# A convolution, attention and expert kernel: both attention stages in fixed orders, and the first image's table in one go

## The chip, the cores and the metric

The kernel runs on one core of one Trainium2 chip. The metric is the device time of the whole program in microseconds (us), the median over several runs. A core has a matrix engine (PE, with its weight loads PEld), a vector engine (DVE), a scalar engine (ACT), a general engine that also issues the indirect transfers (POOL), an engine that issues plain transfers (SP), and 16 DMA engines. TensorE's clock is granted by a throttle, and the profile gives the granted share.

## The reference

Four images of 256 channels and 64 x 64 positions pass two layers, all in float32.

```
x = x + deformable_conv(group_norm(x))        # 3 x 3 taps, offsets and masks from a convolution
t = tokens(x)                                 # 4 x 4096 tokens of 256 channels
t = t + attention(layer_norm(t))
t = t + experts(layer_norm(t))                # 8 experts, the best 2 of each token
```

The convolution samples, for each position and tap, four neighbours with bilinear weights. The attention works across the 4 images, not across positions: for each of 8 heads of 32 channels, the scores of image s against image t are sums over all 4096 positions, the softmax is over the 4 images, and the values are mixed by 4 x 4 numbers for each head, gated by a sigmoid, and projected with a bias. `layer_norm` is applied twice in a row ahead of the projections (once outside, once inside the attention). Experts are a 256 to 256 to 256 network with an exact gelu.

## The kernel before

**Prologue and gathers (layer 0).** Each image gets a table in DRAM, whose rows hold a position and the one below it side by side. `pieces(b)` builds it: group statistics, `block(q)` for each of 8 blocks of 512 positions, which normalizes (`norm`), transposes (`turn`), copies to one of two staging buffers `zt` (`leave`), and issues four stores of 256 KB; the same `block` computes the offsets by a convolution (`rows_of`, `shifted`, `summed`, `kept`), and `positions` turns them into row numbers and weights. For image 0 all this has to be done ahead of the first gather, except the offsets of blocks from `EARLY` = 3 on. Images 1 to 3 are done beside the gathers. `routed` then multiplies the 18 weight blocks of the convolution with the expert router's 8 columns, so that the convolution's products also give its output's router logits; hence rows of `CR` = 264 columns.

The main loop makes 1152 steps (32 tiles of 128 positions x 9 taps x 4 images). In each, POOL issues one indirect gather of 128 rows into one of `NGB` = 10 buffers `g`, ACT and DVE weigh the four corners (`corner0`, `corner`), PE transposes the sum and multiplies it (`product`), adding on the image itself. `done` stores the tokens into `t1` in DRAM in 32 pieces (image b, block j) of 512 tokens. The order of DVE, ACT, PE and POOL is written out by hand here.

**First attention stage.** A loop over 8 blocks of 512 positions j and 4 images b, in an order that the framework's scheduler decides. It loads `t1[b][j]` whole, takes statistics on DVE (`layernorm`), a reciprocal root as a power on POOL (`rstd_of`), and normalizes on DVE:

```
for i in range(NT):
    V.tensor_scalar(dst[:, i, :], src[:, i, :], mv[:, i, 0:1], r[:, i : i + 1], ALU.subtract, ALU.mult)
```

PE transposes it, ACT scales it into the state in SBUF (`channel_major`), PE projects it to q and k (two halves of channels each), ACT copies them. After the four images of a j, DVE makes 32 products `junk<-q,k` that sum up the scores. When all is done a small softmax gives `att`, 4 x 4 numbers for each channel. Ahead of the loop, `routed` multiplies the output weights `wo_sb` with the router, too.

**Second attention stage.** `block(j)` for 8 blocks, in an order that is written out for DVE, ACT and PE. For the four images it does: `value` (two PE projections; for the first image ACT spreads them, scaled, over four buffers `mix`), `mixed` (DVE adds the others), `gate` (a projection and a sigmoid), `gated` (DVE), `output` (PE, 264 columns), `residual` (loads `t1` again and adds the output's bias `bo_sb` on DVE), `added` (DVE, into the state, with a copy to `t2` in DRAM for the first half), then `stats` (DVE `bn_stats` and `bn_aggr`, a power on POOL for each image), `shift`, and `normed` (ACT, into scatter buffers `u`, 6 of them). `pick`, `count` and `placed` choose the two experts and the place of each token in the expert's list. These three for block j-1 run within block j. Then POOL issues 32 scatters of 128 rows for a block, in pieces 14, 4, 4, 5 and what is left. All of block j-1's scatters are issued within block j. After block 4 come `plan(0)` and `fill(0)`, after block 5 `experts_in` (the loads of all expert weights), each in one piece.

**Experts.** 142 tiles of 256 rows, in two halves of the blocks, in a fixed order: rows and weights are fetched, two products each, and the result is scattered back. The last block's `normed`, `pick`, `count`, `placed` and `plan(1)` are put between the first tiles, and its 32 scatters go out one a tile. The tail gathers the two results of each token, weighs, transposes and stores the output.

Of the kernel before, what the change touches and what calls it, by code (L numbers as in the profile page):

```python
# [17 lines left out]
P = 128  # L18
# [14 lines left out]
CR = C + NE  # L33
# [10 lines left out]
EARLY = 3  # L44
# [26 lines left out]
def conv_attn_moe_kernel(  # L71
# [32 lines left out]
    nhalf = const.tile([P, 4], F32, name="nhalf")  # L104
# [28 lines left out]
    def routed(rows, rw, ps_turned, ps_out, pool, name):  # L133


        pr = ps_out.tile([P, len(rows), NE], F32, name=f"{name}_pr", tag="om")
        for n, w in enumerate(rows):
            tp = ps_turned.tile([P, C], F32, name=f"{name}_tp{n}", tag="tp")
            for ch in range(NCH):
                T.transpose(tp[:, ch * P : (ch + 1) * P], w[:, ch * P : (ch + 1) * P], ident)  # L140
            wT = pool.tile([P, C], F32, name=f"{name}_wT{n}", tag="sT")
            S.copy(wT, tp)
            for ch in range(NCH):
                T.matmul(
                    pr[:, n, :], wT[:, ch * P : (ch + 1) * P], rw[:, ch, :],
                    start=(ch == 0), stop=(ch == NCH - 1),
                )
        for n, w in enumerate(rows):
            V.tensor_copy(w[:, C:], pr[:, n, :])

    issued = []

    def in_turn(ins, others):

        for other in others:
            tc.add_manual_dep(
                ins.ins, other.ins.name,
                mybir.DependencyInfo(mybir.DependencyClass.NoSync, mybir.DependencyReason.DATA),
                reason="order of issue",
            )  # L160

    def rstd_of(pool, var, n, name, twice=False, into=None):
# [7 lines left out]
        r = into  # L170
        if into is None:
            r = pool.tile([P, n], F32, name=f"{name}_rstd", tag=f"rstd{n}")
# [26 lines left out]
    with ExitStack() as actx:  # L199
        aw = actx.enter_context(tc.tile_pool(name="a_w", bufs=1))  # L200
        ax = actx.enter_context(tc.tile_pool(name="a_x", bufs=2))
        apad = actx.enter_context(tc.tile_pool(name="a_pad", bufs=2))
        ap_ = actx.enter_context(tc.tile_pool(name="a_params", bufs=2))
        atmp = actx.enter_context(tc.tile_pool(name="a_tmp", bufs=1))
        ag = actx.enter_context(tc.tile_pool(name="a_gather", bufs=1))
        asm = actx.enter_context(tc.tile_pool(name="a_sm", bufs=5))
        ast = actx.enter_context(tc.tile_pool(name="a_stage", bufs=2))
        ps_tp = actx.enter_context(tc.tile_pool(name="ps_tp", bufs=4, space=PSUM))
# [6 lines left out]
        def load_image(b):  # L215
            t = ax.tile([P, NCH, HW], F32, name=f"xraw{b}", tag="xraw")
# [34 lines left out]
        rwc_sb = load_weight(aw, router_w, "rwc_sb")  # L251
# [35 lines left out]
        def pieces(b):  # L287
# [51 lines left out]
            def block(q, at, table=True, offsets=True, alone=False):  # L339
# [9 lines left out]
                def norm(ch):  # L349
                    if ch == 0:  # L350
                        t["xs"] = apad.tile(
                            [P, NCH, RB + 2, W], F32, name=f"xs{b}_{q}{between}",
                            tag=f"xs{between}", bufs=2 if table else 1,
# [7 lines left out]
                    if alone and table:  # L361
                        V.tensor_scalar(to, of, scale, bias, ALU.mult, ALU.add)
                    else:
                        S.activation(to, of, AF.Identity, bias=bias, scale=scale)
# [11 lines left out]
                def leave(i):  # L376
                    if i == 0:
                        t["zt"] = ast.tile([P, NT, C], F32, name=f"zt{b}_{q}", tag="zt")
                    zt = t["zt"]
                    S.copy(zt[:, i, :], t["tp"])  # L380
# [51 lines left out]
                each = 2 if alone else 4  # L432
                if table:
                    for i in range(NT):
                        out_.append((at + each - 1 + each * i, lambda i=i: turn(i)))
                        out_.append((at + each + each * i, lambda i=i: leave(i)))
                sum_at = at + (13 if alone else 18)
                if offsets:
                    for m in range(NCH * 3):
                        rows_at = at + 2 + 2 * m if alone else at + 4 + 2 * m + m // 2  # L440
                        out_.append((rows_at, lambda m=m: rows_of(m)))
                    for kj in range(3):
                        out_.append((sum_at + kj, lambda kj=kj: shifted(kj)))
                    out_.append((sum_at + (3 if alone else 4), lambda: summed(0)))
                    out_.append((sum_at + (4 if alone else 5), lambda: summed(1)))
                    out_.append((sum_at + (5 if alone else 6), kept))
# [100 lines left out]

            place_for()
            for q in range(NBLK):
                first.extend(block(q, n + 6 * q, offsets=False, alone=True))  # L550
            for q in range(EARLY):
                at = n + 9 + 12 * q
                first.extend(block(q, at, table=False, alone=True))
                first.extend(positions(rows_in(q), lambda q=q: of[q], at + 19, 2))
# [19 lines left out]
        ss, tps, sTs, accs, outs, last_corner = {}, {}, {}, {}, {}, {}  # L574
# [5 lines left out]
        def gather(n):  # L580
# [11 lines left out]
            tc.add_to_no_dep_group(buffer, g.ins)  # L592
            return g
# [66 lines left out]
        for when, fn in pieces(0):  # L660
            todo.setdefault(when, []).append(fn)
        routed(
            [wconv_sb[:, ch, k, :] for k in range(K2) for ch in range(NCH)], rwc_sb, ps_tp, ps_om,
            asm, "wconv",
        )
        order = {nc.vector.engine, nc.scalar.engine, nc.tensor.engine, nc.gpsimd.engine}
        with tc.manual_schedule(engines=order):
# [51 lines left out]
        [  # L719
            early_state[:, (j * B + b) * STATE : (j * B + b + 1) * STATE] if j < HB  # L720
            else state_pool.tile([P, STATE], F32, name=f"st{b}_{j}")
            for j in range(NBLK)
        ]
        for b in range(B)
    ]
    t2 = {
# [20 lines left out]
    att_pool = ctx.enter_context(tc.tile_pool(name="att", bufs=1))  # L747
    att = att_pool.tile([P, NCH, B, B], F32, name="att")

# [9 lines left out]
    route_pool = ctx.enter_context(tc.tile_pool(name="route", bufs=1))  # L759
# [4 lines left out]
    rw_sb = load_weight(dw, router_w, "rw_sb")  # L764
# [12 lines left out]
    with ExitStack() as bctx:  # L777
# [7 lines left out]
        wq_sb = load_weight(bw, wq, "wq_sb")  # L785
        wk_sb = load_weight(bw, wk, "wk_sb")
        with ExitStack() as ectx:
            et = ectx.enter_context(tc.tile_pool(name="e_t", bufs=1))
            ps_e = ectx.enter_context(tc.tile_pool(name="ps_e", bufs=1, space=PSUM))
            routed([wo_sb[:, ch, :] for ch in range(NCH)], rw_sb, ps_tp, ps_e, et, "wo")  # L790

            alike = et.tile([P, NCH, P], F32, name="alike")
            V.tensor_copy(alike, bo_c.unsqueeze(2).to_broadcast([P, NCH, P]))
            pb = ps_e.tile([P, 2, NE], F32, name="pb", tag="om")
            for n in range(2):
                for ch in range(NCH):
                    T.matmul(
                        pb[:, n, :], alike[:, ch, :] if n == 0 else ones, rw_sb[:, ch, :],
                        start=(ch == 0), stop=(ch == NCH - 1),
                    )  # L800
            V.tensor_copy(bo_sb[:, C:], pb[:, 0, :])
            V.tensor_copy(rsum, pb[:, 1, :])
# [3 lines left out]
        for j in range(NBLK):  # L806
            qs, ks = [], []
            for b in range(B):
                rows = bt.tile([P, NT, CR], F32, name=f"bt{b}_{j}", tag="t")
                nc.sync.dma_start(rows, t1[b][j])  # L810
                t = rows[:, :, :C]
                layernorm(bs, t, t, f"l1_{b}_{j}", twice=True)
                mn = channel_major(b, j)
                for ch, tp in transpose_in(ps_tp, t, f"tpb{b}_{j}"):
                    S.activation(
                        mn[:, ch, :], tp, AF.Identity,
                        scale=gamma_c[:, ch : ch + 1], bias=beta_c[:, ch : ch + 1],
                    )
                q = bqk.tile([P, NCH, BLK], F32, name=f"q{b}_{j}", tag="qk")
                k = bqk.tile([P, NCH, BLK], F32, name=f"k{b}_{j}", tag="qk")  # L820
                for w, dst, n in ((wq_sb, q, "q"), (wk_sb, k, "k")):
                    for ch in range(NCH):
                        S.copy(dst[:, ch, :], project(ps_mm, w, mn, ch, f"p{n}{b}_{j}_{ch}"))  # L823
                qs.append(q)
                ks.append(k)
            for s_ in range(B):
                for t_ in range(B):
                    for ch in range(NCH):
                        junk = bs.tile([P, BLK], F32, name=f"junk{s_}{t_}{ch}_{j}", tag="junk")
                        V.scalar_tensor_tensor(  # L830
                            junk, qs[s_][:, ch, :], 1.0, ks[t_][:, ch, :],
                            ALU.mult, ALU.mult,
                            accum_out=parts[:, ch, s_ * B + t_, j : j + 1],
                        )


# [82 lines left out]
    ps_s = ctx.enter_context(tc.tile_pool(name="ps_sd", bufs=1, space=PSUM))  # L919

    with ExitStack() as bctx:
        bt = bctx.enter_context(tc.tile_pool(name="d_t", bufs=2))
        ps_mm = bctx.enter_context(tc.tile_pool(name="ps_mmd", bufs=3, space=PSUM))
# [4 lines left out]
        def value(j, t_, ch):  # L928

            if t_ == 0 and ch == 0:  # L930
                for s_ in range(B):
# [3 lines left out]
            pv = pvs[j, t_, ch] = project(  # L935
                ps_mm, wv_sb, channel_major(t_, j), ch, f"pv{t_}_{j}_{ch}"
            )
            if t_ == 0:
                for s_ in range(B):
                    S.activation(  # L940
# [619 lines left out]
```

## Time and profile before

| what | value |
|---|---|
| median of 10 runs | 3576.27 us (3563.69 to 3590.23) |
| profiled execution | 3581.31 us, span 3579.6 us, mean granted clock 0.926 |
| prologue, to the first gather | 0 to 71.6 us |
| gather stage | 71.6 to 2131.4 us |
| first attention stage | 2131.4 to 2444.7 us |
| second attention stage | 2444.7 to 2876.0 us |
| experts while scatters are left | 2876.0 to 3080.0 us, 36 tiles |
| experts after that | 3080.0 to 3508.0 us, 106 tiles |
| tail | 3508.0 to 3579.6 us |

The profile is of one execution; its parts are compared with its own span. "Busy" counts the time in which an engine works on instructions; waiting, issuing transfers and branches are not in it. A wait in brackets names what came last ahead of an instruction. An engine's share over the whole span mixes stages of different kinds, so the shares are read by stage.

### The profile page before, as it was taken

How to read it: one execution, taken by the hardware profiler on the slowest of the kernel's cores; microseconds unless marked ns; L12 is line 12 of the kernel's file. 1: busy time of each engine (PE TensorE's matmuls, PEld its weight loads, DVE VectorE, ACT ScalarE, POOL GpSimd, SP SyncE). 2: the span in 40 equal slices, each digit the busy share in tenths (PEclk: the TensorE clock that was granted, in tenths of full speed). 3: DMA queues.
4: the chain of work that ended last, by engine and by line, in shares of the span. 5: the costliest groups of instructions: out<-in, count | busy, mean ns of one | idle time of the engine just before them, and what ended most of it. 6: DMA issues, size and time to landing. Idle time of an engine off the chain costs nothing. (4 is left out here: it accounts for less than half of the span.)

```text
span 3579.6 us, 49709 instructions
## 1 busy us (share of the span) xinstructions
PE 3069.0 (86%) x13658; PEld 2245.2 (63%) x13658; DVE 2601.5 (73%) x6747; ACT 1723.9 (48%) x3919; POOL 1971.2 (55%) x1800
## 2 busy tenths in 40 slices
PE   6899997889987899977777779897888888999995
PEld 4667666667666577756666654443434467888883
DVE  3767786867776777776666768887888864557777
ACT  3456654556544466544444434443333344556662
POOL 1665666656667666677776741110666655554441
PEclk8899998999998999988888989998999999999996
DMA  8889998899988899987788862112544344547778
GB/s 262 313 303 334 338 334 329 314 354 353 342 320 327 304 361 360 353 306 281 284 298 312 295 252 61 61 49 85 177 158 146 108 124 128 163 125 245 240 242 305
DMA packets 322443, 898.89 MB, mean 251 GB/s; under 512 B 43218, under 2 KB 89949, under 8 KB 320120
## 3 DMA queue, kind: packets, MB, share of 16 engines
q0 software_dynamic: 191808, 671.74, 51.8%
q1 hardware_dynamic: 130360, 223.98, 19.7%
q8 instruction: 113, 1.85, 0.2%
q14 instruction: 162, 1.33, 0.1%
HBM read 744.43 MB, written 154.79 MB: 251 GB/s over the span
## 5 line engine op out<-in xcount | busy, mean ns | idle before, releaser
L606 DVE SCALAR_TENSOR_TENSOR s<-g,wts,s 128x256 f32<-128x256 f32 x3456 | 1432.5, 479 | 530.0 <-ACT s L598 351.1
L582 POOL DMA_INDIRECT g<-table,idx x1152 | 1337.0, 1161 | 755.1 <-DVE s L606 431.7
L645 PE MATMUL acc<-wconv_sb,sT 128*128 128x264 f32 x4608 | 1341.0, 416 | 273.0 <-ACT sT L626 163.9
L645 PEld LDWEIGHTS acc<-wconv_sb,sT 128*128 128x128 f32 x4608 | 837.7, 203 | 418.2 <-ACT sT L626 194.5
L626 ACT COPY sT<-tps 128x256 f32<-128x256 f32 x1152 | 425.7, 370 | 762.5 <-PE tps L620 477.2
L598 ACT ACTIVATE s<-g,wts 128x256 f32<-128x256 f32 x1152 | 588.8, 511 | 218.3 <-DMA g<-table,idx 187.8
L620 PEld LDWEIGHTS tps<-ident,s 128*128 128x128 f32 x2304 | 331.2, 150 | 250.1 <-issue 158.2
L620 PE MATMUL tps<-ident,s 128*128 128x128 f32 x2304 | 462.9, 284 | 25.4 <-DVE s L606 21.5
L1384 POOL DMA_INDIRECT ys_rows<-y,to x284 | 283.2, 997 | 293.3 <-DVE y L1381 225.7
L1110 POOL DMA_INDIRECT xs_rows<-u,slots x256 | 261.6, 1022 | 128.5 <-issue 113.9
L1355 PE MATMUL ph<-xT,w 128*128 128x256 f32 x1136 | 280.8, 390 | 23.7 <-issue 8.2
L1373 PE MATMUL py<-w,hT 128*128 128x256 f32 x1136 | 270.7, 381 | 0.0
L1378 DVE TENSOR_TENSOR y<-py,w 128x512 f32<-128x512 f32 x142 | 98.2, 692 | 204.1 <-ACT w L1317 78.9
L1359 ACT ACTIVATE hT<-ph,w 128x256 f32<-128x256 f32 x284 | 133.7, 474 | 234.1 <-PE ph L1355 171.0
L1355 PEld LDWEIGHTS ph<-xT,w 128*128 128x128 f32 x1136 | 210.0, 195 | 52.9 <-issue 11.1
L1373 PEld LDWEIGHTS py<-w,hT 128*128 128x128 f32 x1136 | 218.0, 192 | 30.4
L173 POOL TENSOR_TENSOR l_rstd<-l_ve,nhalf 128x4 f32<-128x4 f32 x32 | 34.7, 1086 | 250.4 <-DVE l_ve L167 250.4
L830 DVE SCALAR_TENSOR_TENSOR junk<-q,k 128x512 f32<-128x512 f32 x256 | 160.9, 683 | 8.9 <-ACT k L823 8.9
L952 ACT ACTIVATE gate<-pg,bg_c 128x512 f32<-128x512 f32 x64 | 43.8, 686 | 247.4 <-PE pg L753 180.5
L398 PE MATMUL po<-xs,woff_sb 128*96 128x512 f32 x288 | 150.9, 606 | 0.0
L947 DVE SCALAR_TENSOR_TENSOR mix<-pv,att,mix 128x512 f32<-128x512 f32 x192 | 129.7, 741 | 4.3 <-PE pv L753 4.3
L979 PE MATMUL po<-wo_sb,mix 128*128 128x264 f32 x512 | 118.3, 387 | 0.4 <-DVE early_state L993 0.4
(255 smaller groups left out, 3385.6 us busy)
## 6 DMA issues: line engine op xcount, KB each, us to landing
xt<-xs_rows SPq DMA_DIRECT2D x142, 260.0 KB
table<-zt SPq DMA_DIRECT2D x128, 256.0 KB
early_state<-ys_rows SPq DMA_DIRECT2D x128, 256.0 KB
g<-table,idx POOLq DMA_INDIRECT x1152
t<-o SPq DMA_DIRECT2D x32, 528.0 KB
bt<-t SPq DMA_DIRECT2D x32, 528.0 KB
dt<-t SPq DMA_DIRECT2D x64, 264.0 KB
xraw<-in_x SPq DMA_DIRECT2D x16, 1024.0 KB
```

The lines of the kernel that those rows point to most:

```text
L398: T.matmul(t["po"], woff_sb[:, ch, ki].rearrange("p kj o -> p (kj o)"), t["xs"][:, ch, ki : ki + RB], start=(n == 0), stop=(n == NCH * 3 - 1),
L582: g = G.indirect_dma_start(out=gs[n % NGB], out_offset=None, in_=tables[b], in_offset=bass.IndirectOffsetOnAxis(ap=params[b][0][:, r, k : ...
L598: first = S.activation(ss[n], gs[n % NGB][:, :C], AF.Copy, scale=params[b][1][:, 0, r, k : k + 1])
L606: last_corner[n] = V.scalar_tensor_tensor(ss[n], gs[n % NGB][:, c * C : (c + 1) * C], params[b][1][:, c, r, k : k + 1], ss[n], ALU.mult, A ...
L620: T.transpose(tps[n][:, ch * P : (ch + 1) * P], s[:, ch * P : (ch + 1) * P], ident)
L626: S.copy(sTs[n], tps.pop(n))
L645: T.matmul(accs[n // K2][:, :CR], sT[:, ch * P : (ch + 1) * P], wconv_sb[:, ch, k, :], start=False, stop=(k == K2 - 1 and ch == NCH - 1),)
L830: V.scalar_tensor_tensor(junk, qs[s_][:, ch, :], 1.0, ks[t_][:, ch, :], ALU.mult, ALU.mult, accum_out=parts[:, ch, s_ * B + t_, j : j + 1],)
L1110: s = G.indirect_dma_start(out=rows_, out_offset=bass.IndirectOffsetOnAxis(ap=slots[:, k, n : n + 1], axis=0), in_=u[:, n % NT, :], in_off ...
L1355: T.matmul(ph, w1_sb[:, ch, f * P : (f + 1) * P], xT[:, ch, :], start=(ch == 0), stop=(ch == NCH - 1),)
L1373: T.matmul(py[:, i, :], hT[:, f, i * P : (i + 1) * P], w2_sb[:, f, :], start=(f == 0), stop=(f == NCH - 1),)
L1384: s = G.indirect_dma_start(out=ys_rows[g], out_offset=bass.IndirectOffsetOnAxis(ap=to[:, i : i + 1], axis=0), in_=y[:, i, :], in_offset=No ...
```

## The change

It has five parts.

1. The router gets a ninth column of -1/256 (`NX` = 9, `CR` = 265, `load_router`). So every product that gives router logits also gives the negative mean of its row. `routed` becomes a generator that other work can be put between.
2. Prologue: image 0's table is built in one go, with the gather buffers `gs[q]` as staging (8 of the 10). DVE makes every fourth of the copies. The offsets of `EARLY` = 2 blocks follow behind the table, with the router's products of the convolution between them. The pools are reordered, so that the memory of the attention's first rows, weights and states comes free early.
3. First attention stage: an order written out by hand for DVE, ACT, PE and SP. Blocks go j = 4 first, then 0 to 3 and 5 to 7. Loads fetch 256 of the 265 columns. Statistics run two blocks ahead (those of the first block between the last gathers' steps), and the normalization moves from DVE to ACT. Projections are cut into halves that the next block's transposes stand between. Products go four at a time from a list. `with_bias` adds the bias to `t1` in DRAM by one accumulating transfer for each of the 32 pieces, issued by POOL.
4. Second attention stage: a new fixed order. `residual` only loads. `squares` replaces `stats`: ACT squares with a sum for the variance, with the mean from the ninth column. The power and `shift` run for two images at a time. 13 of a block's 32 scatters are left for the next block. `plan(0)`, `fill(0)` and `experts_in` are cut into pieces (`chores`) that go between the work from block 5 on.
5. Start of the experts: `rstd`, `shift`, `normed`, `pick`, `count` and `placed` of the last block at tiles 0 to 5, `plan(1)` from tile 7. 45 scatters are left for the tiles instead of 32.

```
-EARLY = 3
+EARLY = 2
+    def load_router(pool, name):
+        t = pool.tile([P, NCH, NX], F32, name=name)
+        G.memset(t[:, :, NE:], -1.0 / C)
...
                 def leave(i):
                     if i == 0:
-                        t["zt"] = ast.tile([P, NT, C], F32, name=f"zt{b}_{q}", tag="zt")
+                        t["zt"] = (
+                            gs[q].rearrange("p (t c) -> p t c", c=C) if alone
+                            else ast.tile([P, NT, C], F32, name=f"zt{b}_{q}", tag="zt")
+                        )
                     zt = t["zt"]
-                    S.copy(zt[:, i, :], t["tp"])
+                    (V.tensor_copy if alone and i == NT - 1 else S.copy)(zt[:, i, :], t["tp"])
...
+            n += 10 * NBLK + 8
             for q in range(EARLY):
-                at = n + 9 + 12 * q
+                at = n + 20 * q
...
+            for m in range(NCH * K2 + 2):
+                first.append((n + 10 + 1.5 * m, lambda: next(router)))
...
+        def with_bias(b, j):
+            G.dma_start(
+                t1[b][j], bo_sb.unsqueeze(1).to_broadcast([P, NT, CR]), accum_op=ALU.add
+            )
...
+        def normal(n, i):
+            nb, r = norms[n]
+            S.activation(
+                bts[n][:, i, :], bts[n][:, i, :], AF.Identity,
+                bias=nb[:, i : i + 1], scale=r[:, i : i + 1],
+            )
...
+        for n in range(total):
+            more = n + 2 < total
+            if more:
+                statistics(n + 2)
+            multiply(4)
+            projected(n, 0)
+            products(n, 0)
+            if n + 1 < total:
+                turned(n + 1)
+                scaled(n + 1)
+            if n + 3 < total:
+                load(n + 3)
+            if n == 0:
+                routed_output()
+            else:
+                with_bias(*blocks[n - 1])
+            if more:
+                shifted(n + 2)
+                for i in range(NT):
+                    normal(n + 2, i)
+            multiply(4)
+            projected(n, 1)
+            products(n, 1)
+        with_bias(*blocks[-1])
+        multiply(len(pending))
...
         def residual(j, b):
...
                 nc.sync.dma_start(t, t1[b][j][:, i : i + 2])
-                V.tensor_tensor(t, t, bo_sb.unsqueeze(1).to_broadcast([P, 2, CR]), ALU.add)
...
+        def squares(j, b):
...
+                S.activation(
+                    u[:, i, :C], x_[:, i, :], AF.Square, bias=mean[:, n],
+                    accum_out=lns[j, b // 2][:, n % (2 * NT)].unsqueeze(1),
+                )
-        def stats(j, b):
-            x_ = token_major(b, j)
...
-            for i in range(NT):
-                V.bn_stats(st[:, i, :], x_[:, i, :])
-            for i in range(NT):
-                V.bn_aggr(mv[:, i, :], st[:, i, :])
...
         def block(j):
...
+            mixed(j, 1, 1, [2, 3])
+            spread(j, 0, [1, 0])
+            scatter(3)
+            scatter(10)
+            mixed(j, 1, 1, [0])
...
+            scatter(13)
...
+            scatter(5)
...
+            scatter(1)
+            gated(j, 3, 1)
+            squares(j, 1)
...
+            squares(j, 2)
+            added(j, 3, 0)
+            output(j, 3, 1)
+            chore(2)
+            rstd(j, 0)
+            added(j, 3, 1)
+            squares(j, 3)
...
-    at(0, lambda: (shift(last, 3), normed(last, 3)))
-    at(2, lambda: pick(last))
-    at(3, lambda: count(last))
-    at(4, lambda: placed(last))
+    at(0, lambda: (rstd(last, 1), shift(last, 0)))
+    at(1, lambda: (shift(last, 1), normed(last, 0), normed(last, 2)))
+    at(2, lambda: (pick(last), normed(last, 3), normed(last, 1)))
+    at(4, lambda: count(last))
+    at(5, lambda: placed(last))
```

## The prediction

> **What bounds the kernel now.** I first cut the span into stages at the places where the work changes: the first gather, the last product of the convolution, the first value product, the first expert tile. The view by stages then gives each engine's busy time:
>
> ```profile
> core 0: us, PE busy (x) PEld busy (x) DVE busy (x) ACT busy (x) POOL busy (x), PEclk, DMA share, GB/s
> 0.00:71.60 71.60, 41.26 (x171) 26.91 (x172) 31.30 (x104) 27.61 (x61) 6.92 (x20) 0.90 0.81 227
> 71.60:2131.40 2059.80, 1759.08 (x8532) 1353.61 (x8532) 1498.10 (x3715) 1065.75 (x2689) 1343.05 (x1173) 0.92 0.89 322
> 2131.40:2444.70 313.30, 267.99 (x791) 131.87 (x789) 259.22 (x937) 120.74 (x196) 35.26 (x35) 0.94 0.18 58
> 2444.70:2876.00 431.30, 373.34 (x1063) 200.22 (x1064) 360.29 (x959) 149.48 (x323) 259.10 (x244) 0.94 0.44 144
> 2876.00:3080.00 204.00, 170.58 (x791) 143.02 (x789) 104.85 (x261) 93.28 (x176) 117.16 (x118) 0.92 0.41 126
> 3080.00:3508.00 428.00, 417.92 (x2188) 367.67 (x2188) 295.82 (x647) 248.31 (x443) 208.83 (x212) 1.00 0.65 206
> ```
>
> The columns are each engine's busy time, PE's granted clock, the DMA engines' share and their rate. The gather stage is the longest and lives on transfers (share 0.89, 322 GB/s), and no gather's bytes change. Stages three and four, the two attention stages, have two half-hidden engines: PE 86% and DVE 83 to 84%, neither full, so they take turns waiting. ACT is below 40% there. That is where an order can win.
>
> In the first stage I looked in POOL's timeline at what releases the first gather, and at all engines around it, in stages of 5 us with the columns from above:
>
> ```profile
> 71.60 1.21 POOL L582 DMA_INDIRECT g<-table,idx  x1 [50.17 <-DMA table<-zt]
> ```
>
> ```profile
> 70.00:75.00 5.00, 5.00 (x27) 5.00 (x28) 0.00 (x0) 1.28 (x4) 2.78 (x3) 0.50 0.90 326
> 75.00:80.00 5.00, 5.00 (x28) 5.00 (x26) 0.00 (x0) 1.49 (x4) 3.78 (x5) 0.50 0.99 397
> ```
>
> It waits for the table's stores. Their 8.39 MB leave between 24.9 and 67 us, because ACT's copies into the two staging buffers wait for earlier stores.
>
> For the attention stages I read the groups and, for block 3 of the second one, the timelines of POOL, DVE and PE (start, length, engine, line, operation, and in brackets the wait ahead of it):
>
> ```profile
> L830 DVE SCALAR_TENSOR_TENSOR junk<-q,k 128x512 f32<-128x512 f32 x256 | 160.9, 683 | 8.9 <-ACT k L823 8.9
> L173 POOL TENSOR_TENSOR l_rstd<-l_ve,nhalf 128x4 f32<-128x4 f32 x32 | 34.7, 1086 | 250.4 <-DVE l_ve L167 250.4
> ```
>
> ```profile
> 2609.96 0.96 POOL L1110 DMA_INDIRECT xs_rows<-u,slots  x1 [0.30 <-issue]
> 2617.19 0.96 POOL L1110 DMA_INDIRECT xs_rows<-u,slots  x1 [6.27 <-issue]
> ...
> 2659.69 0.17 DVE L1019 SCALAR_TENSOR_TENSOR shift<-l3mv,rstd 128x4 f32<-128x4 f32 x1 [3.21 <-POOL rstd L173]
> ...
> 2670.45 1.98 PE L753 MATMUL pv<-st,wv_sb 128*128 128x512 f32 x4 [0.65 <-DVE mix L947]
> ```
>
> POOL runs 32 scatters a block, then stands 6.27 us with an empty queue; DVE waits 3.21 us for a power that is queued behind scatters; PE waits for DVE's mixes. Blocks repeat every 55 us (their scatters begin at 2617.19 and 2672.30).
>
> **Prologue: -11 us.** With eight gather buffers as staging no copy waits for a store. The rows give 245 GB/s for these stores where the DMA engines were full (243 to 250 GB/s at a share of 0.94 to 0.97), so 8.39 MB need 34 us from 24.9: the first gather starts near 60 instead of 71.6. Behind the table PE now does the offsets and the router's products: 12 matmuls of 512 columns at 0.86 us (10.3), 18 rounds of the router at 1.17 us in the rows above (21.1), small sums 2.1: 34 us from about 37, so it ends at 71. The first gathered rows come 13.7 us after the first issue (71.6 to 85.3, beside the next image's load, which the change leaves beside them): 74. So both chains meet near 74 to 75 against 85.3, and I take 11; bounds 5 (PE slower, bubbles between router and offsets) and 15.
>
> The clock is what could move that. In the rows above PE is busy 5.00 us of 5.00 and is granted only 0.50: 8-column products do not raise the clock. The Trainium skill, "TensorE: Matmul & The Clock Gate", Part 1, says that one busy window of some 3.4 us brings the array to full rate. By the rule the router's rounds, now between wide matmuls, would take half, PE would be done near 61, and the gathers alone would decide; by the row they take 1.17 us. Either way 74 us stands.
>
> **Gather stage: +5 us.** A ninth router column makes 4608 product records 265 columns instead of 264: at 0.2225 us for 264 that is 0.8 ns each, 3.9 us, of which I charge half, since PE only binds where its clock is 1.0. The third offsets block moves from the prologue into the first steps (6 matmuls, 5.2 us of PE in slices where PE has 17% free): nothing, or 5 if that cover is gone. A new wait: the statistics of the first attention block sit in DVE's order at step 861 of 1152, on a load that can only be issued once PE has read image 2's last rows at step 855. A load took 5.4 us to arrive in a quiet stage (issued 2129.50, used 2134.89), six steps are some 10 us, but the gathers crowd the queues; behind it queue the corners of every later step. I take 3, bounds 0 and 8.
>
> **First attention stage: -43 us.** Removed from DVE: 128 normalizations (four in 1.38 us, so 1.38 a block of rows) and the 1.2 us waits for the power before them. Added on ACT: 128 at 0.50, 2.0 a block, beside 3.9 of copies and scales. Sums for one of the 32 blocks: PE two projections of 3.43 and transposes of 1.04: 7.9 us; DVE statistics 1.6, two small ones 0.23, eight products 0.613 apart 4.9: 6.8; ACT 6.0. PE becomes the bound. It needs 253 us; before it took 283.5 from 2143.7 to 2427.1, with a 0.48 us wait for ACT in each block that the new order fills with the other half of the previous projection. The start: before, PE went from its last product (2131.4) to its first projection (2143.7) through a load, statistics and the output's router rows; now the first block's rows and weights are there early, and only two ACT scales stand between: some 3 us, so 9 are saved. The end: 32 products waited for the last keys, 15.4 us; now 12 are left, 7.4. In all 2131.4+3+253+7.4+2.3 = 2397 against 2444.7, 48; I keep 5 back for waits: 43.
>
> What pays for the bias is 32 additions of 541 KB into DRAM, issued by POOL. No row shows one. Issue: a gather with 128 rows takes 0.95+0.30; 512 pieces lie between 1.25 and 5.0, and with the power 1.09 that is at most 6.3 of a 7.9 us block: hidden, as loads land a block ahead. But each addition stands in POOL's order just ahead of its block's power, and waits for its load and for the addition eight back. Transfer: a plain 541 KB store landed in 4.3 us (2131.87 to 2136.2), the load in 5.4; the stage's DMA share of 18% for 32 loads is 1.8 us each. A read and a write make 3.6, both latencies in series 9.7. I take 5, hidden below 7.9. The Trainium skill, "SBUF — State Buffer", Who interferes with whom, speaks against them: a DVE instruction with two SBUF inputs (the products here) takes the read interface that GpSimd needs. The scatters beside an 84% busy DVE ran at a median of 963 ns with 2105 as the longest, so by the row it is small; by the rule issuing might double, and the additions would no longer fit. Bounds of the stage: -55 (all sums met), -15.
>
> **Second attention stage: -50 us.** Leaving DVE a block: 8 residual adds at 0.64 apart, 16 statistics at 0.33, 16 aggregates at 0.08, and half of the small ones: 12 us of 46.6. It keeps 34. ACT gets 16 squares at 0.5 to 0.75: 28 to 31 of its time. PE keeps 32 projection matmuls (64 records of 0.43, 27.5), 64 output records (14.3) and counting (0.65): 42.5. POOL: 32 scatters in 42.8 us (48.8 less four powers) and two powers, 3.2: 46. So POOL takes over, and 13 scatters carried into the next block fill its 6.27 us hole. The two powers wait for the last squares, which wait for a scatter buffer: 1.5 more. Sum: 42 (first block, no scatters), 44, six of 47.5: 371 against 431.3, of which the spreading of plan, fill and expert loads over one block (it took 62 us) is a part. I keep 10 of the 60 back. Bounds: -65, and -20 if the handovers cost what they cost now.
>
> **Experts' start: +10 us.** 45 scatters instead of 32 are left for it, one a tile, 9 tiles longer beyond what it had. Tiles with a scatter took 204/36 = 5.6 us, those after 4.0 (428/106): 9 x 1.6 = 14, less what carried scatters start earlier; bounds 0 and 16. Twelve normalizations on ACT fall here too, in its free half.
>
> **Sum.** -11+5-43-50+10 = -89. The profiled execution took 3581.3 us (span 3579.6), 5.0 above the median of 3576.3. So 3492 for a like execution, 3487 as median.
>
> **Rivals.** (1) Additions bind the first stage. From 7.9 us each they set its pace, through POOL's wait for the eighth before and the power behind it; at 10.7 (7.9+89/32) the whole gain is gone. At 15 us the stage takes 480 instead of 265: 3576+126 = 3700; at 12, 3618. For it: read and write latency in series make 9.7; against: transfers overlap, share 18%. 10%. (2) The second stage keeps its pace: the handovers from DVE to PE and the clock, not DVE's sum, made 55; then -39 remains, 3537. 16%. (3) It does not do what it says: POOL's order defeats both new orders, additions near the limit, and gains cancel with the later scatters: within 10 us of now. 4%. My forecast, all terms near their values, 70%.
>
> A measurement can tell 0.3% (10.7 us). Faster 0.85 (forecast and rival 2, less a little), same 0.04, slower 0.11. Bounds summed: -15+0-55-65+0 = -135 (3441) and -5+13-15-20+16 = -11 (3565); trimmed to 3445 to 3560, which leaves rival 1 out.
>
> **What would show it.** First gather near 60 and first corner near 75; the first attention stage some 265 us with PE over 93% busy and DVE's powers never waited for over 1 us; blocks of the second every 47 us with POOL above 95% counted with its gaps, scatters ending later, near tile 45. Wrong if POOL waits for transfers of the additions, if blocks still take over 52 us, or if the gather stage grows by more than 12.

## The result, and the profile after

The changed kernel takes 3620.56 us (median of 15 runs, 3598.04 to 3657.41) against 3578.94 us for the kernel before (52 runs). The ratio is 1.0107, with a 95% interval of 1.0086 to 1.0129: slower by 1.1%, where 2.5% faster was forecast. The ratio is of the fast runs alone, without two of the changed kernel's that were over 1.5% above its fastest, so it is not quite that of the two medians. The profiled execution took 3595.43 us (span 3593.7), at the lower end of its runs; before's took 3581.31 (span 3579.6).

The view by stages, cut at the same marks as before's (the second attention stage begins with a gate's product now, and is taken to the first transposition of an expert tile, 2882.6 in before). The columns are the stretch, its length, busy time of PE, PEld, DVE, ACT and POOL, PE's granted clock, the DMA share and rate:

```profile
0.00:62.20 62.20, 38.57 (x183) 27.32 (x184) 32.88 (x87) 15.58 (x38) 7.05 (x21) 0.89 0.89 263
62.20:2093.50 2031.30, 1739.93 (x8520) 1326.10 (x8520) 1507.34 (x3751) 1068.63 (x2695) 1307.50 (x1176) 0.94 0.91 327
2093.50:2357.80 264.30, 254.96 (x791) 128.12 (x789) 215.61 (x821) 176.28 (x319) 76.98 (x66) 0.98 0.72 126
2357.80:2885.60 527.80, 376.32 (x1067) 211.15 (x1067) 273.05 (x625) 210.70 (x574) 228.97 (x226) 0.84 0.35 118
```

Before's second attention stage, up to that same mark:

```profile
2444.70:2882.60 437.90, 374.35 (x1066) 200.74 (x1066) 364.86 (x974) 152.59 (x329) 264.53 (x249) 0.94 0.44 143
```

Against before, in us: to the first corner (the first weighing of gathered rows) -13.1 (72.2 after 85.3), from there to the last product -24.8 (2021.3 after 2046.1), first attention stage -49.0 (264.3 after 313.3), second **+89.9** (527.8 after 437.9), experts to the last product +11.4 (632.7 after 621.3), tail -0.2. The sum is +14.2, the difference of the spans to 0.1. All of the loss is in one stage: PE is busy there for about the same time as before (376 against 374 us), DVE for 92 us less, and the stage is 90 us longer. Something keeps both waiting. It is not PE's lower clock (0.84 against 0.94), since PE's busy time has not grown.

The view of waits, for the second attention stage alone (who waited for whom: us in all, times, longest):

```profile
POOL rstd L1170 <- DVE l3var L1168: 206.1, 9, 44.6
ACT gate L1095 <- DVE mix L1110: 155.6, 7, 32.4
PEld pg L791 <- DVE mix L1090: 121.5, 11, 21.7
PE pg L791 <- DVE mix L1090: 108.7, 9, 20.1
DVE mix L1090 <- remote: 104.6, 13, 12.6
```

POOL, ACT and PE wait for DVE's mixes, and the mixes wait for "remote": a release that matches no instruction's end in the records. DVE's timeline in block 2, with PE's and POOL's rows beside it:

```profile
2475.94 0.17 DVE L1256 CAST slots<-row 128x16 int32<-128x16 f32 x1
2483.43 2.72 DVE L1090 SCALAR_TENSOR_TENSOR mix<-pv,att,mix 128x512 f32<-128x512 f32 x4 [7.32 <-issue]
2493.23 2.07 DVE L1090 SCALAR_TENSOR_TENSOR mix<-pv,att,mix 128x512 f32<-128x512 f32 x3 [7.07 <-remote]
2505.84 2.07 DVE L1090 SCALAR_TENSOR_TENSOR mix<-pv,att,mix 128x512 f32<-128x512 f32 x3 [10.54 <-remote]
```

```profile
2470.74 7.11 PE L791 MATMUL pv<-early_state,wv_sb 128*128 128x512 f32 x16
2486.21 3.78 PE L791 MATMUL pg<-early_state,wg_sb 128*128 128x512 f32 x4 [8.36 <-issue]
2507.30 3.78 PE L791 MATMUL pg<-early_state,wg_sb 128*128 128x512 f32 x4 [17.31 <-DVE mix L1090]
```

```profile
2460.62 1.04 POOL L1265 DMA_INDIRECT xs_rows<-u,slots  x1 [0.17 <-issue]
...
2500.03 0.96 POOL L1265 DMA_INDIRECT xs_rows<-u,slots  x1 [0.31 <-issue]
```

The three groups of mixes need the value products that PE's records show as done between 2472.7 and 2477.85. They start at 2483.43, 2493.23 and 2505.84. The trace also has the times at which PE's counter (the semaphore that PE raises when a marked product is done, and on which the mixes wait) rose: after 2474.22 the next recorded ones are 2493.20, 2505.82 and 2505.87, and two of the three groups start within 0.03 us of one. Some rises are missing from this trace (see the last section), but those that released these two groups stand in it. So PE's results came up to 28 us late, and it was not an error of the list of waits. During all of this POOL issues 32 scatters in one row (one after the other, without anything between), from 2460.6 to 2501.0. The rows of the other blocks are alike (32, or 13 and 19 with a short pause between; 19 in block 1), and the blocks, from one last gating product to the next, take 38.0, 52.2, 75.2, 72.5, 72.1, 70.2, 64.3 and 72.8 us; before 41.5, 51.6, 52.8, 54.5, 55.1, 62.1, 53.9 and 54.5.

### The profile page after: what moved, and what is told of

It is laid out like the page before. It is cut to its first block, busy times and chain, and to the rows that moved or that the text cites. A ratio compares the mean times of both kernels' runs of the same rounds, so it can differ in the third digit from the quotient of the medians.

```text
span 3593.7 us, 49649 instructions
## 1 busy us (share of the span) xinstructions
PE 3038.3 (85%) x13658; PEld 2225.1 (62%) x13658; DVE 2476.9 (69%) x6303; ACT 1832.8 (51%) x4281; POOL 1950.0 (54%) x1818
## 3 DMA queue, kind: packets, MB, share of 16 engines
q14 instruction: 161, 1.32, 0.1%
## 4 chain that ended last, share of the span: by engine, by line
PE 36%; issue 22%; POOL 17%; DVE 9%; DMA 7%; another core or an unknown queue 6%; ACT 3%; POOLq 0%; ACTq 0%; SPq 0%; DVEq 0%
PE acc L684 13%; POOL g L620 10%; DMA g<-table,idx 6%; POOL ys_rows L1594 5%; DVE s L645 4%; PE tps L659 3%; PE po L427 3%; PE p_wq_sb L791 3%; PE po L1121 3%; PE p_wk_sb L791 3%; PE pg L791 2%; DVE mix L1090 2%; PE pv L791 1%; DMA early_state<-ys_rows 1%
## 5 line engine op out<-in xcount | busy, mean ns | idle before, releaser
L620 POOL DMA_INDIRECT g<-table,idx x1152 | 1299.2, 1128 | 743.6 <-DVE s L645 454.7
L684 PE MATMUL acc<-wconv_sb,sT 128*128 128x265 f32 x4608 | 1325.3, 412 | 250.1 <-ACT sT L665 129.7
L684 PEld LDWEIGHTS acc<-wconv_sb,sT 128*128 128x128 f32 x4608 | 823.7, 199 | 394.2 <-ACT sT L665 157.9
L1265 POOL DMA_INDIRECT xs_rows<-u,slots x256 | 247.8, 968 | 96.3 <-issue 92.1
L1170 POOL TENSOR_TENSOR rstd<-l3var,nhalf 128x8 f32<-128x8 f32 x16 | 26.5, 1654 | 214.0 <-DVE l3var L1168 206.1
L791 PE MATMUL pg<-st,wg_sb 128*128 128x512 f32 x128 | 74.1, 715 | 79.4 <-DVE mix L1090 73.4
```

Source lines behind the costliest of these rows:

```text
L620: g = G.indirect_dma_start(out=gs[n % NGB], out_offset=None, in_=tables[b], in_offset=bass.IndirectOffsetOnAxis(ap=params[b][0][:, r, k : ...
L684: T.matmul(accs[n // K2][:, :CR], sT[:, ch * P : (ch + 1) * P], wconv_sb[:, ch, k, :], start=False, stop=(k == K2 - 1 and ch == NCH - 1),)
L791: T.matmul(ps, w[:, ci, ch * P : (ch + 1) * P], src[:, ci, :], start=(ci == 0), stop=(ci == NCH - 1),)
L1265: s = G.indirect_dma_start(out=rows_, out_offset=bass.IndirectOffsetOnAxis(ap=slots[:, k, n : n + 1], axis=0), in_=u[:, n % NT, :], in_off ...
```

## Experiments

Theory A: long unbroken rows of POOL's indirect transfers make PE's results late; before had a power after 14, 4, 4 and 5 scatters, the change has one row of 32. Theory B: the new order's own handovers are slow. The experiments ran on three chips, which proved to be the larger finding. They are told apart by what the kernel before took beside them: chip A 3262 to 3265 us, chip B 3522 to 3529, chip C 3574. The result's runs (before 3579) are like chip C's. The kernel before has a kept trace from the result's runs alone.

**Breaks after every fourth scatter (chip A).**

```
+                given.append(s)
+                if not fixed and len(given) % 4 == 0:
+                    pause = bs.tile([P, 4], F32, name=f"pause{len(given)}", tag="pause")
+                    issued.append(G.tensor_tensor(pause, ones[:, :4], nhalf[:, :4], ALU.pow))
+                    in_turn(issued[-1], scattered)
+                    scattered.clear()
```

> The changed kernel; after every fourth scatter of the second attention stage POOL raises four numbers to a power (about 1.04 us, as one of before's powers) before it goes on. Nothing else moves; POOL's work of a block grows from 46 to about 54 us. Theory A: in the changed kernel PE's results come late (DVE's mixes wait 7 to 12 us with nothing to wait for in the records) because POOL issues 32 indirect transfers without a break; before had powers between groups of 4 to 14. Then the blocks fall from 70 to 75 us to 50 to 56, the second stage from 528 to 400 to 440 us, the whole to 3460 to 3510 us. Theory B: the new order's own handovers set 70 us a block. Then the blocks stay at 65 us or more, and the whole stays at 3595 to 3660.

Measured: 3198.97 us against 3262.08, ratio 0.9812 (0.9781 to 0.9843). The numbers expected were for another chip. No wait for "remote" is left in this trace, nor in any other from chip A, with or without breaks, so it settles nothing about A.

**Before's second stage behind the new first stages (chip A).** After's text up to the first attention stage, before's from there; `residual` without its bias addition.

> The changed kernel up to the end of the first attention stage, then before's second attention stage and experts' start (order, statistics on DVE, four powers a block, no carried scatters), without the 64 bias additions, which the transfers into DRAM have done. Both theories put the whole loss into the second stage: 3594 less 528 and 633 plus at most 438 and 621 for before's stages is 3492; with the bias additions gone at 0.64 us each up to 40 less: 3450 to 3500. If the shorter gather stage of the changed kernel's profile (2031 against 2060 us) is chance, 3480 to 3525.

Measured: 3205.84, ratio 0.982 (0.9791 to 0.9849); second stage 420.3 us. Here, too, the range was for the result's chip, and nothing came late.

**Thirty more scatters, or plain stores, in block 0 (chip A).**

```
+        def tries():
+            V.tensor_copy(try_at, try_i)
+            for n in range(30):
+                s = G.indirect_dma_start(out=try_rows, out_offset=..., in_=no_row, in_offset=None)
...
+                s = nc.sync.dma_start(try_rows[n * P : (n + 1) * P], no_row)   # the other kernel
```

> The changed kernel with 30 extra scatters of 128 rows, of constant data into rows that nobody reads, issued by POOL without a break in block 0 of the second attention stage, which has no scatters (38 us from its start to its last gating product). They issue for 38 us. Theory A: DVE's mixes wait for late results of PE in block 0 too, and it grows by 15 us or more. Theory B: block 0 stays at 38 to 42 us.

> The same 30 stores of 128 rows of 1040 bytes in block 0, but issued by SP as plain stores. If it is POOL's issuing that makes PE late, block 0 stays at 38 to 42 us; if it is the transfers themselves, whoever issues them, it grows by 15 us or more as with POOL's scatters.

Measured: block 0 takes 38.2 and 38.0 us, the whole 3167.09 and 3155.84 (one run each). On this chip the scatters do nothing to PE, and the whole is some 100 us faster than before. That made the chip the question.

**The changed kernel and the breaks again (chip A).**

> The changed kernel once more. In the first group of experiments kernels that hold the change ran 55 to 105 us faster than the kernel before (3262 us there, 3579 in the runs of the result), none of PE's results came late in their records, and the second attention stage took 370 us with 30 extra transfers in it. Theory C: the change gains what was forecast where PE's results come in time, and loses where they come late under long unbroken rows of indirect transfers. With before near 3262 the changed kernel takes 3140 to 3160; with before near 3579 it takes 3600 to 3640 again. Rival: the changed kernel is slow by itself: slower than before in both.

> The changed kernel with a power on POOL after every fourth scatter of the second attention stage, once more. With before near 3262 (PE's results in time) the breaks only cost: POOL needs 54 us a block and binds it, 40 to 50 us more than the changed kernel. With before near 3579 (results late) theory A expects 3460 to 3530 against 3620 for the changed kernel; theory B, own handovers, 3595 to 3660.

Measured: the changed kernel takes 3153.46 us against 3264.62, ratio **0.9668** (0.9639 to 0.9698); with breaks 3192.39, ratio 0.9778 (0.975 to 0.9807). On chip A the change gains 111 us, where 89 were forecast. Its second stage, with the same columns as above:

```profile
2112.90:2482.10 369.20, 348.18 (x1066) 200.77 (x1067) 271.16 (x625) 209.29 (x574) 233.28 (x226) 0.98 0.50 168
```

PE is busy 94% of it, and the clock is granted at 0.98. The breaks cost 39 us there, since POOL then needs 54 us a block.

**Breaks after every eighth scatter, and no additions into DRAM (chip B).** The first is the edit above with 8 for 4. The second leaves `with_bias` empty and adds the bias on DVE in `added`.

> The changed kernel with a power on POOL after every eighth scatter of the second attention stage: 4 powers a block, 45.5 us of POOL's work instead of 40.5, within the 42.5 to 54 us that a block took where PE's results came in time. Theory A with the two bounds of theory C: with before near 3264 it costs 0 to 15 us against the changed kernel's 3153; with before near 3579, where rows of up to 14 scatters in the kernel before showed hardly any late result and rows of 19 and 32 did, it takes 3470 to 3560 against 3620. Rival: the breaks change nothing there (3600 to 3640).

> The changed kernel without the 32 accumulating transfers in the first attention stage; DVE adds the bias in the second one just ahead of each addition of the output (64 additions of about 0.64 us, 5.1 us a block). Forecast's reading, the additions are hidden: the first stage stays at 258 to 264 us, and the second grows by 0 to 40 us, since DVE then has 39 us of a 42.5 us block. Its rival 1, the additions cost: the first stage falls by over 10 us without them.

Measured, beside 3528.53 for before: with breaks **3443.22**, ratio 0.9764 (0.9738 to 0.979); without the additions, and with the rows of 32, 3551.0, ratio 1.0061 (1.0031 to 1.0091). The range for the breaks was for a before of 3579; the gain of 85 us over before lies within the 19 to 109 that it stands for. The waits of the second stage, first of the kernel with unbroken rows, then of the one with breaks:

```profile
POOL rstd L1169 <- DVE l3var L1167: 196.2, 9, 46.0
ACT gate L1093 <- DVE mix L1108: 150.1, 7, 30.8
PEld pg L791 <- DVE mix L1088: 130.2, 10, 25.6
PE pg L791 <- DVE mix L1088: 119.5, 8, 24.8
DVE mix L1088 <- remote: 95.6, 8, 16.8
```

```profile
POOL xs_rows L1265 <- issue: 67.6, 192, 12.9
PEld pv L791 <- issue: 57.3, 236, 0.5
POOL rstd L1170 <- DVE l3var L1168: 55.3, 7, 44.5
...
DVE st L1138 <- remote: 24.5, 8, 5.8
...
DVE early_state L1138 <- remote: 11.6, 6, 3.6
```

The mixes' wait is gone, and the stage falls from 517.5 to 399.1 us. DVE's additions of the output still wait 36.1 us for late results: eight scatters are still 10 us of issuing. The two differ in the additions, too, but the kernel with SP's stores below has both the additions and the unbroken rows, and its second stage takes 520.7 us on this chip. (The changed kernel without an edit was not run on chip B.) So 118 to 122 us hang on four small POOL instructions a block, which theory B can't explain; nor can it explain chip A, where the same order runs in 369 us. The first attention stage is 262.7 us with the additions into DRAM and 264.3 without: they cost nothing, as forecast.

**Breaks in the gather stage too, and block 0 again (chip B).**

```
                     gather(n + NGB + 1)
+                    if n % 8 == 0:
+                        G.tensor_tensor(pause_, ones[:, :4], nhalf[:, :4], ALU.pow)
```

> The kernel with a power after every eighth scatter, and also a power on POOL after every eighth gather of the gather stage (144 powers, 150 us of POOL's work in a stage where it is busy 1300 of 2010 us). Theory A: where PE's results come late (before near 3530 or 3580), rows of 16 to 20 gathers make ACT wait some 115 to 190 us for PE's transposes in the gather stage too; with rows of 8 the stage falls from 2010 to 1850 to 1980 us and the whole to 3300 to 3420. Theory D: gathers are bound by the transfers, the late results there are caught up: 2000 to 2030 us. Where results come in time (before near 3264): 1790 to 1830 us, up to 40 us more than without.

> 30 extra scatters without a break from POOL in block 0 of the second attention stage of the changed kernel, once more. With before near 3530 or 3580 theory A expects block 0 at 55 us or more (38 without them); with before near 3264, 38 us again.

> The same 30 stores in block 0, issued by SP as plain stores. With before near 3530 or 3580: block 0 stays at 38 to 42 us if POOL's issuing makes PE's results late, and grows to 55 us or more if the transfers do, whoever issues them.

Measured: block 0 takes **53.6** us with POOL's 30 scatters, just short of the 55 expected, and **37.9** with SP's 30 stores of the same bytes (the whole 3571.39 and 3569.57, one run each). DVE's timeline in block 0, first with POOL's scatters, then with SP's stores:

```profile
2361.67 2.07 DVE L1090 SCALAR_TENSOR_TENSOR mix<-pv,att,mix 128x512 f32<-128x512 f32 x3 [5.88 <-remote]
2377.88 0.69 DVE L1138 TENSOR_TENSOR early_state<-po,dt 128x512 f32<-128x512 f32 x1 [7.79 <-remote]
```

```profile
2369.34 2.07 DVE L1090 SCALAR_TENSOR_TENSOR mix<-pv,att,mix 128x512 f32<-128x512 f32 x3 [0.45 <-PE pv L791]
2377.68 0.68 DVE L1138 TENSOR_TENSOR early_state<-po,dt 128x512 f32<-128x512 f32 x1
```

The same mixes wait 5.88 us for "remote" in one and 0.45 for PE's recorded end in the other; the first addition waits 7.79 us for "remote" in one and not at all in the other. The scatters wrote constant rows that nobody reads, and the same program takes 38.2 us for this block on chip A, so no data dependency can be behind it; and it isn't the bytes. The kernel with breaks in both stages takes 3407.27 us against 3522.15, ratio **0.9673** (0.9606 to 0.974): the fastest on this chip, though the interval touches that of the breaks in the second stage alone. Its gather stage takes 1976.9 us, against 2010.6 with breaks in the second stage only (2007 to 2019 in the four traces of this chip without breaks there), and ACT's wait for late transposes there falls from 125.2 to 89.4 us. That is the lower end of the 30 to 160 us that theory A allowed; most of the 222 us by which this stage was longer than on chip A (1788.1) is not explained by rows of over eight, and 189 are left.

**The changed kernel, before's second stage, and two kinds of rows (chip C).** The first scatters' kernel with a power after every fourth, and a kernel in which POOL issues the 30 stores without an index (`G.dma_start(try_rows[n * P : (n + 1) * P], no_row)`).

> The changed kernel beside the ones with breaks on a chip where before takes 3520 to 3580. Theory A: 3550 to 3590 with before near 3525 (blocks 1 to 7 of the second stage at 60 to 73 us, as in the kernel with 30 plain stores). With before near 3264: 3140 to 3160 again.

> The new prologue and first attention stage with before's second stage, whose POOL work has powers after 14, 4, 4 and 5 scatters. With before near 3525, theory A: second stage 420 to 440 us as in before, the whole 3430 to 3470. If late results come with the new first stages in any case, 3500 or more. With before near 3264: 3206 again.

> The 30 extra scatters in block 0 with a power after every fourth: 45 us of POOL's work. With before near 3525, theory A: block 0 back at 38 to 43 us, against 53.6 without the breaks. If it is the number of scatters and not the unbroken row, 50 us or more.

> The 30 extra stores in block 0 issued by POOL, but as plain stores without an index. With before near 3525: 50 us or more for block 0 if any row of transfers issued by POOL makes PE late, 38 to 42 us if only indirect ones do.

Measured, beside 3574.43 for before: the changed kernel 3610.18, ratio 1.0091 (1.0059 to 1.0123), the result over again; with before's second stage **3507.91**, ratio 0.9803 (0.977 to 0.9836), its second stage 439.7 us against 526.4. The wholes in these two ranges were for a before of 3525, and this chip's is 49 us above that; the second stage, forecast at 420 to 440, decides, and no wait for "remote" lies in it. The prologue and the first attention stage gain on either sort of chip. Block 0 takes 37.8 us with 30 scatters in groups of four (the whole 3604.34, one run): 30 scatters do no harm with seven powers between them, so it is the unbroken row. The 53.6 us without powers are chip B's; on chip C the unbroken 30 were not run, but in this very trace the later blocks, whose rows are unbroken, take 60 to 75 us. Block 0 takes 38.2 us with POOL's plain stores (the whole 3578.22, one run). But those issue in 18 us (2348.9 to 2367.0) instead of 38, no longer than the rows of 14 in before; whether a longer row of plain stores would do harm is open.

## Why the prediction was wrong

**The step that failed** is in the second attention stage: "So POOL takes over, and 13 scatters carried into the next block fill its 6.27 us hole." The sum of POOL's work was right, but it was taken as a cost on POOL alone. Before's four powers stood between the scatters; now two powers come together ahead of rows of 13 to 32 scatters, PE's results come late beside these, and the stage went to 527.8 us instead of 371. That the powers between the scatters keep the results in time is shown (399.1 us on chip B with four back in each block); whether POOL's hole helped, too, no run tells. On chip A, where rows do no harm, the stage takes 369.2 us, with blocks of 37.7, 42.5, 42.5, 45.3, 45.7, 48.1, 54.3 and 42.5 us. There the prediction's terms show: PE is busy throughout blocks 1, 2 and 7, whose 42.5 us are its sum, and blocks 3 to 5, in which POOL hardly pauses, lie near the 46 to 47.5 of POOL's. That the total comes to 2 us is partly luck: the blocks sum to 358.6, and 10.6 us after the last gating product were in no term.

**The rivals.** None named this. Rival 1 (additions bind the first stage) is refuted: the 32 additions are 40.0 us of POOL's busy time, 1319 ns each as a mean, and the stage is as long without them. (Its prices do not fit each other, either: 10.7 us for no gain and 3618 at 12 give 3714 at 15, not 3700.) Rival 2 had the place right, "handovers from DVE to PE", and would not go beyond the old 55 us a block; the handover was worse than before, not as before. "Wrong if blocks still take over 52 us" named the sign of failure, not its cause.

**The evidence was in before's profile.** Its view of waits for the gather stage has this line:

```profile
ACT sT L626 <- remote: 191.6, 60, 7.8
```

A wait of 191.6 us, in 60 places, which no record ends, is a resource that nobody has named. I did not read it. Of the 44 rises of PE's counter in that stage that come over 3 us after the last recorded end, 32 lie in rows of 16 to 20 gathers (under 0.5 us between them) or within 6 us behind one, stretches that make up some 38% of the stage. A look at where they lie would have pointed at long rows, though only the experiments could show them to be the cause, and would have given the range its upper side.

**The terms that held.** Prologue: -13.1 to the first corner, forecast -11; the first gather starts at 62.2 (forecast near 60). In stages of 5 us, with the columns from above, PE works on the offsets and the router behind the table:

```profile
50.00:55.00 5.00, 5.00 (x17) 3.16 (x16) 1.32 (x7) 1.89 (x3) 0.00 (x0) 0.50 0.93 259
55.00:60.00 5.00, 5.00 (x17) 3.24 (x18) 1.45 (x10) 0.37 (x1) 0.00 (x0) 0.50 0.91 256
60.00:65.00 5.00, 5.00 (x17) 3.18 (x16) 0.42 (x1) 0.37 (x1) 2.20 (x2) 0.50 0.99 345
```

It is granted 0.50 for 15 us while busy all the time by these rows, with wide products between the router's small ones. So the trace again speaks against the rule of the Trainium skill ("TensorE: Matmul & The Clock Gate", Part 1) by which a busy window gives the full rate, as far as the rows' busy time, whose ends are modelled, can be trusted.

First attention stage: -49.0, forecast -43, PE busy 96% of it; the other waits there were smaller than the 5 us kept for them, though DVE waited for powers in 8 places, up to 3.7 us, where none over 1 us was forecast. The rule on the shared interface of DVE and GpSimd (the Trainium skill, "SBUF — State Buffer", Who interferes with whom) is for GpSimd instructions that read SBUF. It does not show in the issuing of these additions, 1.32 us each beside DVE's products, so the prediction stretched it. Experts: +11.4, forecast +10.

**Gather stage:** -24.8 in the profiled pair, forecast +5, with 0 and 13 in the sum of the bounds. On chip C the changed kernels' stages were 2067.1, 2054.9, 2041.9 and 2019.5 us with the same instructions up to there, so a single profile can't resolve 5 us in it. The new wait for the first statistics took 2.1 us (DVE at 1577.5), forecast 3. The reading that this stage "lives on transfers" was too strong: on chip A the same bytes pass in 1788 us, at 370 GB/s and a share of 0.97 (in the kernel with 30 scatters), against 322 and 0.89 here.

## What to carry to other kernels

Read the waits that end on nothing before the ones that end on an engine: they are where a resource is hidden. Small instructions between one engine's transfers can be what lets a neighbour's results come in time; before moving them away, look at what the neighbours do during an unbroken row. Cut rows of indirect transfers by a small POOL instruction after every eight (399 against 517 and 521 us for the stage on chip B; on chip A breaks after every fourth cost 39 us), and time a change on more than one chip: this one was 3.3% faster on chip A and 1% slower on chip C.

## What the runs showed of the hardware

On the result's chip and on B and C, PE's results come late beside POOL's indirect transfers issued back to back, one every 1.27 us. In one of the longest rows (2460.6 to 2501.0) the first rise of PE's counter that is over 1 us late comes 11.5 us after the row's begin, and the last 4.8 us after its end. One power of 1.04 us after four (block 0, chip C) or eight (the whole stage, chip B) of them prevents most or all of it; a kernel with breaks in the whole stage was not run on chip C, nor among the result's runs. The rows of 14 scatters in the kernel before show no rise over 3 us late. On chip A no row of any length did this. In all traces of these chips DVE's and ACT's recorded rises are at most 0.5 us late, but for the last two at the program's end; only PE's are late. The recorded ends of PE's products can precede the moment at which they are of use by up to 28 us, so a busy or idle PE in the records of such a stretch is not to be trusted. Whether PE computes late or only reports late, these runs do not tell.

The chips differ in one more thing that the traces show: on chip A the changed kernel's trace has a rise for each of PE's 2422 marked ends, on the result's chip 1983 and on chip C 1981. The missing ones lie beside POOL's indirect transfers: on the result's chip 941 of 1206 are there in the gather stage and 178 of 204 in the second attention stage, but 322 of 322 in the first, which has none. During the 30 scatters of block 0 on chip B 8 of 16 are there, and in that block 21 of 21 with SP's stores. DVE's and ACT's are thinned out in the same places. So indirect transfers disturb the records on just those chips on which results come late. Every run on record lists a span and a granted clock of its own, so none is known to have run untraced, and that the tracing has a part in the lateness is not excluded.
